# A conditioning vector on its way through DRAM: 1536 single numbers, or 16 rows turned by TensorE

## The chip, the core and the metric

The kernel runs on one core of one Trainium2 chip. The metric is the device time of one execution in microseconds (us); less is better. The engines are TensorE (PE, with its weight loads as PEld), VectorE (DVE), ScalarE (ACT), GpSimd (POOL) and SyncE (SP). SP issues nearly all DMAs here; its entries in a timeline (SPq) are the time that the issue of a DMA took, not the transfer itself.

## The reference, cut to what matters

`x` is 4 batches of 1024 tokens of 512 numbers, `cond` has one row of 128 numbers for each batch.

```python
scale = cond @ norm_w.T + 1.0                       # [4, 512]
ms = jnp.mean(x * x, axis=-1, keepdims=True)
h = x * (scale[:, None, :] * jax.lax.rsqrt(ms + 1e-6))
u = h @ up_w.T                                      # [4, 1024, 4096]
val, gate = jnp.split(u, 2, axis=-1)
h = val * gelu(gate)                                # exact gelu
y = act_quant(h) @ weight_quant(down_w).T           # 8 bits a token; three values
return y + x
```

The change concerns `scale`: how its rows for batches 1 to 3 get from the layout in which they are computed to the layout in which the tokens are multiplied by them.

## The kernel before, in words

Work goes batch by batch, in a schedule written out by hand (`manual_schedule`): each engine carries out its instructions in the order in which the program text issues them, and waits on semaphores where data or a buffer is not ready. The up product is cut into NJ = 16 blocks j of 128 columns of `val` and 128 of `gate`, and into two halves h of 512 tokens.

**The first batch.** `plain_half(j, h)` (line 600) makes one block of one half: 12 matmuls of the gate into a PSUM bank `pg` (line 580), a gelu by ACT (line 604), 12 matmuls of the value into `pv` (line 580), and DVE's product of the two (line 608). `pg` has one bank for h = 0 and two in turn for h = 1; `pv` has two in turn, so a `pv` group waits until DVE's line 608 of two groups before has read the bank. The order of the halves is (1,0), (2,0), (0,1), (1,1), (2,1), and then (3,0), (3,1), (4,0), (4,1) and on to (15,1), by the loop at line 1176, which calls `first_batch(j, sc)` (line 1020).

**Weights on the fly.** Between the halves of block j, the other engines prepare later blocks. `w_range` (line 282) finds a row's power of two on DVE (lines 271, 147, 277, 280); `w_scale` (line 293) scales by it, on ACT from block 3 on (line 298). From block 3 on, `w_rows(n)` (line 317) splits the block into a high and a low f16 part (ACT line 322, DVE line 323) in a slot of the buffer `H`, and SP's transposing DMA of line 324 turns it into the weight tile: one of two tiles in `SXY`, or `S_more`, a part of `R`, for every third block (5, 8, 11, 14). The slot serves again two blocks later: ACT's line 322 of block 7 waits until the transpose of block 5 has been read out. POOL adds the block's quarters for the later batches (`s_sums`, lines 356 to 359), ACT and POOL split the sums (lines 368 and 372), and SP spills them to DRAM (`s_spill`, line 376). In `first_batch(j)` the text order between the halves and after them sets what stands behind what; `w_rows(5)` stands between the halves of j = 3, `w_rows(6)` after its second half, `w_rows(7)` after the second half of j = 4.

**The down weights.** `d_sum` (line 427), `d_mean` (the `pmean` matmul of line 436 at the end of j = 4), `d_round` (DVE, lines 442 and 443) and `d_put` (ACT line 452) quantize `down_w` in the same stretch.

**The conditioning.** `scT` [128, NK, B] holds `scale` with the 512 numbers of a batch as 4 columns (NK = 4) of 128 partitions, for 4 batches (B). Batches 1 to 3 are computed by `cond_scale_rest` (lines 189, 190), `cond_largest` adds 1 (line 194) and finds the largest of each batch, `cond_over` turns these on PE (`pm`, line 203), `cond_range` and `cond_spread` make a power of two of each and spread it over the partitions (`pd`, line 219), and `cond_undo` stores it and its inverse (`dx`, `ux`, lines 223 and 226). This last part, followed by `cond_rows` (line 228), runs in `first_batch(3)`, after its first half and ahead of two `pair_max` on DVE (line 694) and of `w_scale(5)` and `w_rows(5)`. `cond_rows` writes the columns of each batch b to a DRAM tile `rows_dram` [B, 512], one DMA for each batch, 512 runs of 4 bytes in it.

At j = 5, `cond_load_scale(1)` reads the row back, to all 128 partitions (line 236), as tile `sc`; at j = 6 `cond_bring` multiplies it by `ux` (DVE line 240), and the tokens of batch 1 are multiplied by it in the blocks 6 to 13 (`Tokens`: `norm` line 499 and `rsqrt` lines 469 and 470, `scale` lines 507 and 512, `sums` on POOL from line 520, then a split, lines 544 and 548, and a transposing DMA, line 551). The rows of batches 2 and 3 are read the same way at the start of batches 1 and 2, and used on line 240 some blocks later.

**Later batches.** They use 7 products of half the size for 8 (line 565, a Strassen form), with the quantization and the down product of the batch before beside them (line 836).

Of the kernel before, what the change touches and what calls it, by code (L numbers as in the profile page):

```python
# [8 lines left out]
F32 = mybir.dt.float32  # L9
# [9 lines left out]
P = 128  # L19
# [31 lines left out]
def glu_quant_kernel(  # L51
# [10 lines left out]
    PE, ACT, DVE, POOL, SP = nc.tensor, nc.scalar, nc.vector, nc.gpsimd, nc.sync  # L62
    B, S, D = x.shape
# [5 lines left out]
    NK = D // P  # L69
# [6 lines left out]
    sm = ctx.enter_context(tc.tile_pool(name="small", bufs=2))  # L76
# [3 lines left out]
    ident = cpool.tile([P, P], F32, name="ident")  # L80
# [28 lines left out]
    warm = H[:, 9, 0].bitcast(F16)[:, :TOK]  # L109
    DVE.memset(warm, 0.0)  # L110
    am_dram = tc.dram_tile([B, 2 * TOK], F32, name="am_dram")
    rows_dram = tc.dram_tile([B, D], F32, name="rows_dram")

    def t_view(b):
        v = R[:, b % 2].bitcast(F16)[:, : NA * C_ALL * 2 * HALF]
# [33 lines left out]
    def bank(tag, bufs, shape=None, name=None):  # L149
        return psum.tile(shape or [P, TOK], F32, name=name or tag, tag=tag, bufs=bufs)  # L150

    def po_bank(name, shape=None):
        return bank("po", 3, shape, name)


    scT = cpool.tile([P, NK, B], F32, name="scT")
# [70 lines left out]

    def cond_rows():

        for b in range(1, B):  # L230
            SP.dma_start(out=rows_dram[b].rearrange("(k p) -> p k", p=P), in_=scT[:, :, b])

    def cond_load_scale(b):

        sc = wpool.tile([P, D], F32, name=f"sc_{b}", tag="sc", bufs=1)
        SP.dma_start(out=sc, in_=rows_dram[b].partition_broadcast(P))
        return sc

    def cond_bring(b, sc):
# [780 lines left out]
    def first_batch(j, sc):  # L1020
# [19 lines left out]
        if j == 3:  # L1040
            pd = cond_spread(dg, 1, B, "po")
            cond_undo(pd, 1, B)
            cond_rows()
# [132 lines left out]
    for j in range(3, NJ):  # L1176
        if j == 5:
            sc = cond_load_scale(1)
        if j == 6:
            cond_bring(1, sc)  # L1180
        first_batch(j, sc if j >= 5 else None)
# [87 lines left out]
    for b in range(1, B):  # L1269
# [19 lines left out]
        if b + 1 < B:  # L1289
            sc = cond_load_scale(b + 1)  # L1290
            bring = lambda b=b, sc=sc: cond_bring(b + 1, sc)
            steps[1, "z"] = [(bring, (0.4, 0))]
            p0 = b * NJ + 12
            plan = [
                (None, p0, ((6, "z"), (7, "x"), (7, "y"), (9, "y"), (10, "x"), (10, "z"))),
                (p0 + 4, None, ((9, "y"), (10, "x"), (10, "y"), (11, "y"), (12, "x"), (12, "x"))),
                (None, None, ((10, "y"), (11, "x"), (11, "y"), (13, "x"), (13, "y"), (13, "z"))),
                (p0 + 2, p0 + 4, ((9, "z"), (12, "x"), (12, "y"), (14, "x"), (14, "y"), (14, "z"))),
            ]
            for a, (at, nx_at, places) in enumerate(plan):  # L1300
                def make(a=a, at=at, nx_at=nx_at, b=b):
                    toks[a] = Tokens(b + 1, a, at, nx_at)
                    toks[a].load()
                fs = [
                    make,
                    lambda a=a: toks[a].norm(),
                    lambda a=a, sc=sc: toks[a].scale(sc),
                    lambda a=a: toks[a].high(),
                    lambda a=a: toks[a].low(DVE),
                    lambda a=a: toks[a].turn(),  # L1310
                ]
                costs = ((0, 0), (0, 1.6), (0, 1.5), (0, 2.1), (2.6, 0), (0, 0))
                for place, f, c in zip(places, fs, costs):
                    steps.setdefault(place, []).append((f, c))
# [85 lines left out]
    b = B - 1  # L1400
# [159 lines left out]
```

## Time and profile before

| What | us |
|---|---|
| median of 3 runs | 738.65 (738.46 to 740.53) |
| the profiled execution | 738.87 |
| its span, first to last instruction | 737.1 |
| PE busy (matmuls) | 722.0 (98%) |
| DVE, ACT, POOL busy | 596.9, 391.3, 199.0 |
| first batch on PE, `plain_half` and `plain_first` | to 194.25 |
| a group of 12 matmuls of line 580, full clock, start to start | 2.59 |
| rows written, line 231: 3 DMAs of 2 KB, issue to landing | 10.9 |
| `sc` read, line 236: 3 DMAs of 256 KB, issue to landing | 5.4 |

In the chain of work, a view that goes back from the last instruction and notes what released each step, the share of an engine is the time in which it was the one that the end waited for. Where PE is in the chain nearly all the time, another engine's time counts only where PE stands still for it. The table of the page in 40 slices of 18.4 us shows the granted clock of PE (PEclk) in tenths: 9 in 39 slices and 8 in the fifth, 73.7 to 92.1 us. The list of DMA packets gives, for any stretch of time, how many packets started in it and how many of them were small.

### The profile page before, as it was taken

The numbers are of one execution on the slowest core, as the hardware profiler recorded it, in microseconds if no ns is written. First come the engines' busy times: TensorE is split into PE (matmuls) and PEld (weight loads), VectorE is DVE, ScalarE is ACT, GpSimd is POOL, SyncE is SP. The second block draws the span as 40 slices with busy tenths as digits, with TensorE's granted clock in tenths as the row PEclk, the third lists the DMA queues.
The fourth block names the chain that finished last, engine by engine and source line by source line (L and its number), as shares of the span: only waits on it lengthen the run. The fifth ranks groups of instructions, "written<-read, shape, count | busy, mean of one in ns | idle before, by whom it ended". The sixth has DMA issues, their size and how long they took to land.

```text
span 737.1 us, 10140 instructions
## 1 busy us (share of the span) xinstructions
PE 722.0 (98%) x3660; PEld 359.2 (49%) x3660; DVE 596.9 (81%) x827; ACT 391.3 (53%) x629; POOL 199.0 (27%) x207
## 2 busy tenths in 40 slices
PE   7998799999999999999999999999999999999998
PEld 3544344444444445665444445666444444445844
DVE  6978889876979889797689897787678888764897
ACT  6868476665235676534334666453433666332274
POOL 1379757896110030460010030452020000000100
PEclk9999899999999999999999999999999999999999
DMA  6659999998434646866944556766934565453263
GB/s 239 242 181 206 277 243 235 260 262 221 150 87 106 134 106 155 196 150 180 223 105 101 99 131 171 157 152 162 225 101 103 103 106 107 102 104 97 86 187 114
DMA packets 204382, 117.30 MB, mean 159 GB/s; under 512 B 166950, under 2 KB 174503, under 8 KB 204332
## 3 DMA queue, kind: packets, MB, share of 16 engines
q1 hardware_dynamic: 204042, 116.33, 64.9%
q8 instruction: 28, 0.46, 0.3%
q10 hardware_dynamic: 290, 0.33, 0.1%
q14 instruction: 22, 0.18, 0.1%
HBM read 54.22 MB, written 23.09 MB: 105 GB/s over the span
## 4 chain that ended last, share of the span: by engine, by line
PE 90%; DMA 3%; DVE 2%; POOL 2%; ACT 1%; issue 1%; SPq 0%; DVEq 0%; POOLq 0%; ACTq 0%
PE A L565 34%; PE E L565 17%; PE B L565 8%; PE po L836 8%; PE pg L580 8%; PE pv L580 7%; PE po_end L785 4%; DMA R<-H 2%; PE po L785 1%; DMA H<-in_x_dram 1%; DMA SXY<-H 1%; POOL R L372 1%; PE po_B L836 0%; PE ptx L926 0%; PE pv L623 0%
## 5 line engine op out<-in xcount | busy, mean ns | idle before, releaser
L565 PEld LDWEIGHTS <-SXY 128*128 128x128 f16 x2016 | 197.3, 98 | 232.3 <-issue 0.6
L565 PE MATMUL A<-R,SXY 128*128 128x512 f16 x1152 | 266.2, 379 | 0.0
L565 PE MATMUL E<-R,SXY 128*128 128x512 f16 x576 | 140.0, 379 | 0.1
L663 DVE SCALAR_TENSOR_TENSOR H<-A,sg,t 128x512 f32<-128x512 f32 x48 | 36.0, 750 | 72.9 <-PE A L565 72.7
L715 POOL PARTITION_ALL_REDUCE am<-R x8 | 14.4, 1795 | 232.2 <-DVE R L701 232.2
L757 DVE TENSOR_TENSOR H<-H,am 128x1024 f32<-128x1024 f32 x64 | 76.2, 1217 | 0.0
L580 PEld LDWEIGHTS <-SXY 128*128 128x128 f16 x486 | 47.3, 98 | 58.1 <-DMA SXY<-H 0.8
L676 ACT ACTIVATE t<-t,sg 128x512 f32<-128x512 f32 x48 | 34.6, 721 | 70.7 <-DVE t L673 70.6
L565 PE MATMUL B<-R,SXY 128*128 128x512 f16 x288 | 70.0, 379 | 0.0
L699 DVE TENSOR_REDUCE gm<-H 128x512 f32<-128x1024 f32 x56 | 69.0, 1232 | 1.0
L580 PE MATMUL pg<-R,SXY 128*128 128x512 f16 x252 | 57.8, 379 | 0.3 <-DMA SXY<-H 0.3
L836 PE MATMUL po<-wd,R 128*128 128x256 fp8e4 (+1 forms) x448 | 56.8, 275 | 0.0
L580 PE MATMUL pv<-R,SXY 128*128 128x512 f16 x234 | 54.4, 379 | 0.4 <-DVE H L608 0.4
L836 PEld LDWEIGHTS <-R 128*128 128x128 bf16 (+1 forms) x480 | 46.9, 98 | 12.8
L660 ACT ACTIVATE t<-B,sg 128x512 f32<-128x512 f32 x48 | 33.0, 688 | 35.8 <-PE B L565 35.8
L469 POOL TENSOR_SCALAR ssq<-ssq 128x2 f32<-128x2 f32 x12 | 3.6, 299 | 176.7 <-ACT xt L499 124.0
L643 ACT COPY t<-A 128x512 f32<-128x512 f32 x48 | 28.0, 583 | 39.8 <-PE A L565 39.5
L651 ACT COPY B<-A 128x512 f32<-128x512 f32 x48 | 27.4, 572 | 39.0 <-PE A L565 38.5
L765 ACT ACTIVATE H<-H 128x1024 f32<-128x1024 f32 x38 | 39.9, 1050 | 14.2 <-DVE H L757 14.1
L655 ACT COPY v<-E 128x512 f32<-128x512 f32 x48 | 28.1, 586 | 31.6 <-PE E L565 27.8
L580 PEld LDWEIGHTS <-R 128*128 128x128 f16 x258 | 25.6, 100 | 37.2 <-DMA R<-H 6.0
L701 DVE TENSOR_TENSOR R<-R,gm 128x512 f32<-128x512 f32 x56 | 42.6, 762 | 1.3
(203 smaller groups left out, 999.1 us busy)
## 6 DMA issues: line engine op xcount, KB each, us to landing
SXY<-s_dram SPq DMA_DIRECT2D x57, 256.0 KB, 3.2
s_dram<-SXY SPq DMA_DIRECT2D x18, 384.0 KB, 3.2
H<-in_L_cond_up_w_dram SPq DMA_DIRECT2D x13, 512.0 KB, 5.1
SXY<-s_dram SPq DMA_DIRECT2D x39, 128.0 KB, 3.3
xr<-in_x_dram SPq DMA_DIRECT2D x19, 256.0 KB, 3.6
out_dram<-xr SPq DMA_DIRECT2D x19, 256.0 KB, 2.5
H<-in_x_dram SPq DMA_DIRECT2D x8, 512.0 KB, 6.7
R<-in_L_cond_down_w_dram SPq DMA_DIRECT2D x8, 512.0 KB, 7.3
```

The lines of the kernel that those rows point to most:

```text
L565: PE.matmul(o, s[:, w, k, :], tv[:, :, c, l, k, :], start=start and n == 0, stop=stop and n == len(TERMS) - 1, skip_group_check=True,)
L580: PE.matmul(ps, a[k // 2][:, w, k % 2, :], XP[:, l, k, h * TOK : (h + 1) * TOK], start=n == 0, stop=n == len(terms) - 1,)
L655: ACT.copy(cur["v"], cur["E"])
L660: ACT.activation(cur["t1"], pb, AF.Gelu, scale=gain(g, 1))
L663: DVE.scalar_tensor_tensor(h_half(g - 1, 0), prev["A"], gain(g - 1, 0), prev["t1"], ALU.mult, ALU.mult)
L676: ACT.activation(prev["t2"], prev["t2"], AF.Gelu, scale=gain(g - 1, 1))
L699: DVE.tensor_reduce(gm[0], v, AX.X, ALU.max, apply_absolute_value=True)
L701: return [largest, lambda: DVE.tensor_tensor(m, m, gm[0], ALU.max)]
L757: DVE.tensor_tensor(v, v, r.to_broadcast([P, 2, TOK]), ALU.mult)
L765: ACT.activation(v, v, AF.Copy, bias=MAGIC)
L785: PE.matmul(po.rearrange("p (y c o) -> p y c o", c=2, o=P), q[:, a, h, j], wd8[:, :, j // n, j % n, :, y0:y1].rearrange("p c o y -> p y c o"),
L836: PE.matmul(po, w[:, j], m, start=start and j == 0, stop=stop and j == n - 1, skip_group_check=True,)
```

## The change

`cond_rows` no longer writes columns. PE turns `scT`, seen as [128, 16] (column k * B + b), into [16, 128] in a PSUM bank of the kind `po` (three in turn); DVE copies it to SBUF; SP writes it with one DMA, 16 rows of 512 bytes. `rows_dram` has the shape [16, 128] for it, and the load of a batch takes its four rows of 128 numbers to each partition, 4 runs of 512 bytes where one of 2048 was. The place in the program, the numbers and everything after the load are as before; the column of batch 0 goes along and is not read.

```diff
-    rows_dram = tc.dram_tile([B, D], F32, name="rows_dram")
+    rows_dram = tc.dram_tile([NK * B, P], F32, name="rows_dram")
...
     def cond_rows():
 
-        for b in range(1, B):
-            SP.dma_start(out=rows_dram[b].rearrange("(k p) -> p k", p=P), in_=scT[:, :, b])
+        pr = po_bank("pr", [NK * B, P])
+        PE.transpose(pr, scT.rearrange("p k b -> p (k b)"), ident)
+        rows = sm.tile([NK * B, P], F32, name="rows", bufs=1)
+        DVE.tensor_copy(rows, pr)
+        SP.dma_start(out=rows_dram, in_=rows)
 
     def cond_load_scale(b):
 
         sc = wpool.tile([P, D], F32, name=f"sc_{b}", tag="sc", bufs=1)
-        SP.dma_start(out=sc, in_=rows_dram[b].partition_broadcast(P))
+        SP.dma_start(
+            out=sc.rearrange("p (k q) -> p k q", k=NK),
+            in_=rows_dram.rearrange("(k b) q -> b k q", b=B)[b].partition_broadcast(P),
+        )
         return sc
```

## The prediction

> **What bounds the kernel now.** I read the page's chain of work first, then the waits, the timeline of the stretch they point to, then the DMA packets in it. The chain's share by engine:
>
> ```profile
> PE 90%; DMA 3%; DVE 2%; POOL 2%; ACT 1%; issue 1%; SPq 0%; DVEq 0%; POOLq 0%; ACTq 0%
> ```
>
> TensorE (PE) sets the end, so only time in which it stands or runs slowly can be won. The list of PE's waits names one of size:
>
> ```profile
> PE pg L580 <- DMA R<-H: 5.9, 1, 5.9
> PE pv L580 <- DVE H L608: 0.4, 1, 0.4
> ```
>
> The chain in order of time (start, us, what) shows that wait. The DMA is the transposing one of line 324, which `w_rows(5)` issues; before and after, PE's groups of 12 matmuls take 2.59:
>
> ```profile
> 63.88 0.95 PE pv L580 x5
> 64.84 12.82 DMA R<-H
> 77.66 0.04 issue
> 77.70 4.63 PE pg L580 x12
> 82.33 2.59 PE pv L580 x12
> ...
> 103.09 0.70 ACT g L604
> 103.79 0.01 issue
> 103.80 1.23 DVE xn L512
> ```
>
> PE had finished everything older at 71.77 (the `pmean` matmuls, 71.49 + 0.28) and stood 5.93 until 77.70. The windows by time give a granted clock of 0.50 from 75 to 81, back at 1.00 from 82: the first group after the wait took 4.63, 2.04 more than its neighbours. The episode costs PE 5.93 + 2.04 = 7.97 us. Another transpose on this line, from 45.93, lies 4.37 long in the chain; why did this one take 12.82? SP's queue shows what went just ahead, and what SP then did:
>
> ```profile
> 63.03 1.69 SPq L231 DMA_DIRECT2D rows_dram<-scT  x3
> 64.84 2.98 SPq L324 DMA_TRANSPOSE R<-H  x1
> 67.92 1.00 SPq L376 DMA_DIRECT2D s_dram<-SXY  x2
> 69.01 0.41 SPq L376 DMA_DIRECT2D s_dram<-R  x1
> 69.53 10.48 SPq L324 DMA_TRANSPOSE SXY<-H  x1
> ```
>
> The three writes of the rows are the change's subject. The DMA packets of three single microseconds, 58 to 59 (an undisturbed transpose), 66 to 67 and 69 to 70:
>
> ```profile
> DMA packets 1001, 0.26 MB, mean 256 GB/s; under 512 B 1001, under 2 KB 1001, under 8 KB 1001
> ...
> DMA packets 1924, 0.13 MB, mean 125 GB/s; under 512 B 1911, under 2 KB 1911, under 8 KB 1924
> ...
> DMA packets 31, 0.01 MB, mean 8 GB/s; under 512 B 31, under 2 KB 31, under 8 KB 31
> ```
>
> The small packets pass in the microsecond from 66; afterwards the transpose, which had run at 1001 packets per us, crawls at 31 to 163 from 68 to 74 and recovers at 74 to 75 (675). The row of the writes says 10.9 us from issue to landing: 64.22, the last one's issue, + 10.9 = 75.1, where the crawl ends. So I hold the 1536 four-byte writes to DRAM for its cause. Against "any small packets do this": reading `am_dram` back as single numbers puts 790 small packets into 242 to 243, and those reads land in 3.1 us.
>
> **The change, part by part.** Blocks are written (j, half).
>
> Removed: three writes, 1.69 us of SP, 1536 packets. Added on PE: one f32 transpose behind the `pd` matmuls at 55.63. The row of `pm` on line 203, of the same kind, has 0.27 and 0.42; I take 0.3. It waits for nothing (`scT` is final at 39.04). Added on DVE: one copy of 16x128 out of PSUM behind `dx` (61.22). Rows around it: a COPY of 128x3 at 0.13, a 3x128 reduction out of PSUM at 0.27, a TENSOR_SCALAR of 128x12 at 0.34; no row is of its kind, so 0.13 to 0.34, and I take 0.27. Its wait on PE is over by 56.4, five us before DVE comes there; behind it stand the two L694 and L323 of w_rows(5), and with L323 the transpose at 64.84, which DVE released (L323 ended at 64.77; SP was free at 64.73). So transpose (5) goes out at 65.1, not earlier, although SP has 1.2 us less to issue. DVE then idled 1.25 before 66.69, so the copy's cost ends there. The write's wait on the copy (done near 61.7) is over before SP is through with line 263 at 62.99.
>
> The write of 16 rows has no row: from below 2.0 us to landing (128 KB of results), from above 10.9. Its only reader is the load at 91.25, over 20 us later: nothing, either way. The three loads of `sc` fall from 128 packets of 2048 bytes to 512 of 512. Between the rate of 256-byte packets (256 GB/s, 58 to 59) and of 2048-byte ones (395, 84 to 85) 256 KB take 1.02 or 0.66 us: 0 to 0.4 more on the first load (nearer 0.2); the others are issued far ahead of their use (the last at 363.7, line 240 at 382.8).
>
> Here the skill speaks against the change. "DMA: Bandwidth & Descriptors", section "Why small descriptors are slow (HBM only)", charges a packet some 3 extra cycles and 32 bytes of metadata; by that alone 1536 packets over 16 engines are gone in well under a microsecond, and removing them would save about that. The packets did pass in about one microsecond here, but the rows show eight more during which others stood. "Specifications" of the same page puts full rate at 512 bytes and up; by it the loads lose nothing.
>
> Now the saving. Transpose (5) issued at 65.1 + 4.4 (median landing of line 324) = 69.5, before PE's 72.1 (71.77 + 0.3). PE's wait and the slow clock go: 7.97 - 0.3 = 7.7 at most. **What is late next** decides how much stays. I replay the engines' orders with their own row durations.
>
> ACT's L322 of w_rows(7) waited for the same landing (77.73 after 4.73 idle): it now starts at 73.05, ends 74.1. DVE's L323 (7), at 78.81 after 1.68 idle, starts when L438 ends at 77.14, ends 78.4; what follows on DVE moves 1.7. POOL's sums (L356 to L359, ending 76.79) did not depend on PE, so ACT's L368 (6) goes to 75.7, POOL's L372 from 79.59 to 76.8. ACT's two L452 wait for the rounding on DVE (L443), the second until 83.8; then come g (5,1) at 84.9 (87.55 before), L368, L298, and L322 (8) ending 88.95 (91.57). DVE's L323 (8) follows and ends at 90.7, not 93.3. Before, DVE then stood 2.92 for `sc`, until 96.23. On SP, transpose (6) no longer blocks 10.48 (others 1.9 to 4.9), SP is free by 73 to 75, and transpose (7) goes out behind L323 (7), at 78.45 and not 83.61. With the same issue times behind it, the load of `sc` moves from 91.25 to 86.1 and lands (4.98, plus up to 0.4) at 91.1 to 91.5; with a shorter issue of (7), earlier. So `cond_bring` on line 240 starts between 90.7 and 91.5: 5.5 to 4.7 earlier, 5.3 taken. From there DVE is busy to L512 (103.80), POOL takes it up at 105.10 after 8.35 idle, and the chain runs POOL, ACT, DVE to L608 (9,0) and PE's 134.53: all of it 5.3 earlier. PE comes out of its lead: it now waits about 1.7 at pv (6,0) for L608 (5,0) (85.6 + 0.74), and again near 112 and 129; there it stands where the chain lets it, 5.3 earlier than before. After 134.53 PE waits 0.6 in all in the old trace, so the shift reaches the end. The other loss of the old wait, 2.4 us, is given back to that chain.
>
> Sum: the profiled execution took 738.87 (span 737.1 and 1.77 around it); 738.87 - 5.3 = 733.6. It lies 0.22 above the median of the runs (738.65), so 733.4.
>
> **Rivals.** (a) The chain behind it is looser than my replay (POOL's and DVE's durations vary between 0.72 and 1.2 for one form): then PE's own rate binds, 738.65 - 7.7 = 731.0. For it: PE waited 0.39 for others in the whole stretch; against it: the chain of 103 to 134. (b) The chain is tighter: only ACT's 2.65 at g (5,1) survives, because `sc` lands late or the DMA queue, busy to the full around 85 to 105, moves its work less: 738.65 - 2.65 = 736.0. (c) The change doesn't do what it says: the crawl has another cause (two transposes and three spills in flight), or 16 rows hold up the queue as well. Then the wait stays and 0.3 on the transpose's issue is added: 739. Against it: none of this line's 12 other transposes shows more than about 1 us of such a crawl in its packets, and it ends where the writes land. (d) Slower: PE's new waits between 84 and 130 each drop the clock as the old one did. The episode at 0.50 lasted some 6.8 us (0.3 of the microsecond from 74 by its 0.84, six full ones, 0.5 of the one from 81 by its 0.74), worth 3.4 at most; it must first use up the 2.4 of slack and the 5.3, so it decides from three episodes on (10.2), and four give 738.65 - 7.7 + 13.6 = 744.6. Against it: the wait of 1.6 ahead of the `ptx` matmuls at 10.6 left the clock at 1.00, and none of the new ones in the replay is longer than 1.7.
>
> **How the numbers follow.** Forecast, 732.5 to 734.8: 0.55. (a), 730.9 to 732.5: 0.14. (b), 734.8 to 736.8: 0.22. (c): 0.06. (d): 0.03. A difference of 0.3%, 2.2 us, is about what a measurement of this kernel can tell from none, so faster means under 736.4: 0.55 + 0.14 + 0.20 = 0.89; same 0.08 ((c) and the end of (b)); slower 0.03. The range takes (a) and (b) up to their own prices: 731.0 to 736.2.
>
> **What would show it.** Right: no PE wait on `R<-H`, the clock at 1.00 from 74 to 82, transpose (5) landing in 4 to 6, no one-microsecond window under 200 packets between 67 and 72 while a transpose is out, transpose (6) issued in under 5; line 240's start near 91; PE waits on L608 of 1 to 2 near 85 and a smaller one near 129. Wrong: a wait on `R<-H` that stays (c); PE unbroken from 72 to 195 (a); line 240 at 93 or later (b); clock below 1 after 84 (d).

## The result, and the profile after

| | before | after |
|---|---|---|
| median (lowest to highest) of 11 runs each | 738.61 (737.21 to 740.85) | 736.39 (735.1 to 737.82) |
| ratio | | 0.9967, interval 0.9953 to 0.9982 |
| the profiled execution, its span | 738.87, 737.1 | 735.1, 733.3 |

The change makes the kernel 2.2 us faster. The forecast was 733.4, and 736.39 lies 0.2 above the range's upper end. The profiled execution of after is the fastest of its eleven; profile against profile the gain is 3.8. So there are two things to explain: why 3.8 and not 5.3, and why 2.2 in the medians.

Lines of the changed kernel are 6 higher from line 237 on (L324 is now L330, L240 is L246, L608 is L614, L512 is L518); `rows` is copied on L233, written on L234 and read back on L239. The chain of work by engine, and the granted clock, on the page of after:

```profile
PEclk9999999999999999999999999999999999999999
...
PE 84%; DVE 9%; ACT 2%; issue 2%; POOL 1%; DMA 1%; SPq 0%; DVEq 0%; ACTq 0%
```

The fifth slice is at 9 now, so the slow clock after the wait is gone. PE's share of the chain fell from 90 to 84 and DVE's rose from 2 to 9: in a stretch DVE has become the engine that the end waits for. PE's waits (in total, times, longest) say where:

```profile
PE pv L586 <- DVE H L614: 2.9, 3, 1.8
...
PE pmean L442 <- DVE wpart L437: 0.8, 1, 0.8
```

No wait on `R<-H` is left. Three new ones on DVE's line 614 stand in its place (0.74 ahead of 86.74, 1.78 ahead of 114.64, 0.38 ahead of 130.72). SP's timeline shows that the transposes are free:

```profile
63.25 0.44 SPq L234 DMA_DIRECT2D rows_dram<-rows  x1
66.42 1.89 SPq L330 DMA_TRANSPOSE R<-H  x1
...
70.63 3.46 SPq L330 DMA_TRANSPOSE SXY<-H  x1
```

Transpose (6) blocks SP for 3.46 instead of 10.48. The packets of two microseconds, 68 to 69 and 69 to 70, belong to transpose (5); there is no crawl (before: 51 and 31):

```profile
DMA packets 833, 0.21 MB, mean 213 GB/s; under 512 B 833, under 2 KB 833, under 8 KB 833
...
DMA packets 832, 0.21 MB, mean 212 GB/s; under 512 B 832, under 2 KB 832, under 8 KB 832
```

Where did the rest of the gain stay? Two timelines of after side by side, first DVE (start, us), then POOL in the same stretch:

```profile
87.38 2.02 DVE L449 TENSOR_SCALAR R<-R 128x1024 f32<-128x1024 f32 x1
89.32 0.74 DVE L614 SCALAR_TENSOR_TENSOR H<-pv,sg,g 128x512 f32<-128x512 f32 x1
89.98 1.71 DVE L329 TENSOR_TENSOR H<-H 128x1024 f16<-128x1024 f32 x1
91.62 0.95 DVE L246 TENSOR_SCALAR sc<-sc,ux 128x512 f32<-128x512 f32 x1
```

```profile
86.64 2.22 POOL L378 TENSOR_TENSOR SXY<-H,SXY 128x768 f16<-128x768 f32 x1 [1.88 <-ACT SXY L374]
...
90.58 1.71 POOL L363 TENSOR_TENSOR H<-H 128x256 f32<-128x256 f32 x1
```

And the same two DVE lines before:

```profile
88.72 0.69 DVE L443 TENSOR_SCALAR R<-R 128x1024 f32<-128x1024 f32 x1
...
96.23 0.49 DVE L240 TENSOR_SCALAR sc<-sc,ux 128x512 f32<-128x512 f32 x1 [2.92 <-DMA sc<-rows_dram]
```

The rounding took 0.69 when it began ahead of POOL (whose L372 started at 89.03), and takes 2.02 behind POOL's 2.22, which began at 86.64. The multiplication of `sc` took 0.49 and takes 0.95 behind POOL's 1.71. It no longer waits for `sc`: it follows L329 without a pause, so DVE's own work is what sets it.

### The profile page after: what moved, and what is told of

Read it like the earlier page. It is cut to its first block, busy times and chain, and to the rows that moved or that the text cites. A ratio compares the mean times of both kernels' runs of the same rounds, so it can differ in the third digit from the quotient of the medians.

```text
span 733.3 us, 10144 instructions
## 1 busy us (share of the span) xinstructions
PE 721.2 (98%) x3661; PEld 358.5 (49%) x3661; DVE 600.6 (82%) x828; ACT 390.9 (53%) x629; POOL 200.1 (27%) x207
## 4 chain that ended last, share of the span: by engine, by line
PE 84%; DVE 9%; ACT 2%; issue 2%; POOL 1%; DMA 1%; SPq 0%; DVEq 0%; ACTq 0%
PE A L571 34%; PE E L571 17%; PE B L571 8%; PE po L842 8%; PE pv L586 5%; PE pg L586 5%; PE po_end L791 4%; DVE H L614 1%; DVE H L329 1%; DVE wam L277 1%; PE po L791 1%; DVE R L448 1%; DMA H<-in_x_dram 1%; DVE gm L705 1%; DVE nx L554 1%
## 5 line engine op out<-in xcount | busy, mean ns | idle before, releaser
L688 DVE SCALAR_TENSOR_TENSOR H<-v,sg,t 128x512 f32<-128x512 f32 x48 | 36.6, 762 | 7.4 <-ACT t L682 7.4
```

The costliest lines, as they stand in the source:

```text
L688: DVE.scalar_tensor_tensor(h_half(g - 1, 1), prev["v"], gain(g - 1, 0), prev["t2"], ALU.mult, ALU.mult)
```

## The experiments

Executions start differently: the first loads land earlier or later, and PE's wait ahead of the `ptx` matmuls (1.4 in the profile of after, up to 3.4 in others) carries that on. To compare one profile with another I use the time from the start of PE's group (3,0), which lies ahead of what nearly all variants change, to the end of DVE's last instruction, with which the chain ends. It is 683.95 before and 680.02 after.

**1. Before again, unchanged.**

> The kernel before, unchanged, to see its own executions one by one: span and granted clock of each. Theory A (the missing part of the gain is the new copy on DVE): executions near 738.6, all with a clock near 0.995, as the profiled one, and a wait on R<-H of 5 to 6 in the profile. Rival B (the profiled execution of before was a dear one: how long the clock stays low differs from execution to execution): times spread over 737.2 to 740.9 with the clock, from 0.998 down to 0.991, and the cheapest executions are those with the shortest low clock. Rival C (the changed kernel's new waits lower its clock): says nothing on this run.

Measured: 739.02 (12 runs), ratio 0.9993 (0.9981 to 1.0005). Its profile starts 1.16 later, at (3,0) in 51.51 and not 50.35, and still has the span 737.0:

```profile
PE pg L580 <- DMA R<-H: 4.6, 1, 4.6
PE ptx L926 <- DVE wam L147: 2.6, 1, 2.6
```

PE leaves the wait at 77.50, against 77.70 in the first profile. The transpose, from 66.09 to 77.46, was 11.37 long here and 12.82 there. From (3,0) to the end it is 682.68, 1.27 less. The shorter crawl is 0.61 of that: DVE's line 512 (`xn`), through which the chain runs, starts 52.84 after (3,0) here and 53.45 there. The other 0.66 is a wait of PE near 330, of 0.6 on line 836, which the first profile has and this one lacks. Behind `xn`, fourteen of the seventeen profiles take 630.46 to 630.63 to the end, and the three without that wait (this one and those of runs 8 and 14) 629.70 to 629.85. Two differences between executions are mixed here, then, and `xn` shows the crawl alone.

The equal span in spite of the late start doesn't show that the old wait swallows one. The transpose went out 14.58 after (3,0) here and 14.49 there, so its issue moved with the start, and what made up for it is the shorter crawl and the missing wait. Run 7, which has the crawl too, starts 1.95 later than the first profile and has a span 1.9 longer.

**2. No turn and no copy.** The write takes 16 rows of the identity, so the scales of batches 1 to 3 are left out.

```diff
-        pr = po_bank("pr", [NK * B, P])
-        PE.transpose(pr, scT.rearrange("p k b -> p (k b)"), ident)
-        rows = sm.tile([NK * B, P], F32, name="rows", bufs=1)
-        DVE.tensor_copy(rows, pr)
-        SP.dma_start(out=rows_dram, in_=rows)
+        SP.dma_start(out=rows_dram, in_=ident[: NK * B])
```

> The change without its turn: the one write of 16 rows of 512 bytes takes the identity's first 16 rows, PE's transpose and DVE's copy are left out, so batches 1 to 3 get wrong scales; everything else as in the changed kernel. Theory A (the copy on DVE and what it shifts cost about 0.9): cond_bring on DVE starts near 90.7 instead of 91.6, the transpose of block 5 goes out near 65.0 instead of 66.4, median about 0.9 below the changed kernel, 735.5. Rival C (clock lowered by PE's new waits): same time as the changed kernel, 736.4, within 0.4, and the clock below 1 in about two executions of three.

Measured: 735.36 (8 runs), ratio 0.9943 (0.9923 to 0.9963); 679.68 from (3,0). The turn and the copy together cost 0.34 by that measure, and 0.34 at `xn` too (49.20 after (3,0) and not 49.54; the profiles of the change and of runs 5, 8 and 12 to 15 lie between 49.54 and 49.62). The median is 1.0 lower, as far as the expectation had it, but it says more of the starts: 2 of these 8 executions have a mean clock of 0.998 or less, and 5 of the change's 11.

**3. The copy on ACT.**

```diff
-        DVE.tensor_copy(rows, pr)
+        ACT.copy(rows, pr)
```

> The changed kernel with the copy of the 16 rows out of PSUM on ACT instead of DVE. Theory A: ACT has room there (it idles before w_rows(7) and later), so it runs like the kernel without the turn: 735.5 to 735.9, transpose of block 5 out near 65.2. Rival C: 736.4, as the changed kernel.

Measured: 736.87 (9 runs), ratio 0.995 (0.9932 to 0.9968); 679.74 from (3,0), 0.28 less than the change. The median doesn't show it: this profile had a start gap of 2.68 and a clock of 0.5 for 3.41 from 12.87 on.

**4. The turn, the copy and the write early:** the call leaves `first_batch(3)` and stands ahead of the loop, behind the `pm` matmul at about 39.

```diff
-            cond_rows()
...
+    cond_rows()
```

> The changed kernel with the turn, the copy and the write of the rows moved up to just behind the pm transpose (they need scT alone, which is ready at 39), where DVE idles 2.2 and 2.6 before 49. Theory A: the copy costs nothing there; transpose of block 5 out near 65.0, cond_bring near 90.7, median 735.5. Rival C: 736.4, as the changed kernel.

Measured: 736.69 (8 runs), ratio 0.9954 (0.9936 to 0.9971); 679.65 from (3,0), and the same kind of start (gap 2.26, clock 0.5 for 6.83 from 12.47 on). Runs 2 to 4 agree: taking the copy off DVE's way gives about 0.3, so it is not where 1.4 to 2.6 us of the forecast went.

**5 and 6. Twice the idle matmuls at the start,** in the changed kernel and in the one before.

```diff
-    keep_warm(7)
+    keep_warm(14)
```

> The changed kernel with 14 instead of 7 idle matmuls on PE behind the pd matmul of the start, in PE's gap from 9.3 to 10.7 (up to 11.8 in executions whose first loads land late). Theory D (executions of both kernels sometimes drop the clock near 12.5, behind that gap, which costs 1.3 to 2.5; without such a drop the change gains 3.5): clock 1.0 in nearly all executions, median 735.4. Rival E (what hurts is the late landing of the first loads, which the old wait on the transpose swallowed and the changed kernel pays): the median stays near 736.4, with a clock of 1.0 all the same.

Measured: 735.98 (735.28 to 736.35, 5 runs), ratio 0.9956 (0.994 to 0.9971), every run with a mean clock of 1.0; 680.05 from (3,0).

> The kernel before with the same 14 idle matmuls. Theory D: clock 0.995 (the drop behind the wait on the transpose stays) in nearly all executions, none at 0.993 or lower, median 738.6 to 738.9, 3.3 above the changed kernel with them. Rival E: 738.9 as well, but then 2.4 above the changed kernel with them.

Measured: 738.96 (11 runs), ratio 0.9995 (0.9983 to 1.0007); 682.79 from (3,0), PE's wait on `R<-H` 4.20. With 14 idle matmuls in both, 3.0 separate the medians of the two. The changed kernel's median goes from 736.39 to 735.98. The old one's stays (738.70 beside it with 7), although none of its 11 executions has a mean clock below 0.995; why it gains nothing is open.

**7. The change, with three writes of single numbers put back,** to a DRAM tile that nobody reads.

```diff
+        for b in range(1, 4):
+            SP.dma_start(out=junk_dram[b].rearrange("(k p) -> p k", p=P), in_=scT[:, :, b])
```

> The changed kernel, and behind its one write of the rows the three old writes of columns, 1536 numbers of 4 bytes, to a DRAM tile that nobody reads. Theory A (these writes alone hold up the transposing DMA): the transpose of block 5 lands 11 to 13 after its issue, PE waits 4 to 7 on R<-H, the clock falls, 738.5 to 739.5. Rival F (the crawl came of the turn of other DMAs in flight): no wait on R<-H, the time of the changed kernel.

Measured: 740.81 in one run. PE's wait, and SP's queue:

```profile
PE pg L589 <- DMA R<-H: 5.4, 1, 5.4
```

```profile
65.55 1.53 SPq L237 DMA_DIRECT2D junk_dram<-scT  x3
67.19 1.92 SPq L333 DMA_TRANSPOSE R<-H  x1
...
71.39 10.20 SPq L333 DMA_TRANSPOSE SXY<-H  x1
```

The packets from 70 to 71:

```profile
DMA packets 39, 0.01 MB, mean 10 GB/s; under 512 B 39, under 2 KB 39, under 8 KB 39
```

The wait, the crawl and the clock of 0.5 for 6.83 are back as they were, and from (3,0) it took 684.00, like the kernel before. The rest of the 740.81 is a late start (ahead of `ptx` a wait of 2.52, then a clock of 0.5 for 3.41). So it was these writes.

**8. The same 1536 packets of 4 bytes to SBUF instead.**

```diff
+        for b in range(1, B):
+            SP.dma_start(out=junk_sb[:, b, :, 0], in_=scT[:, :, b])
```

> The changed kernel, and behind its one write of the rows three DMAs with the same source columns, 1536 packets of 4 bytes again, but to a strided tile in SBUF. Theory A1 (it is single numbers written to DRAM that back up): the packets pass in a microsecond or so, the transpose of block 5 lands 4 to 6 after its issue, no wait on R<-H, 735 to 736.5. Rival A2 (so many packets of 4 bytes hold up the queue wherever they go): a wait on R<-H of 4 to 7, 738.5 to 739.5.

Measured: 734.44 in one run, no wait on `R<-H`. The packets from 66 to 67 and from 68 to 69:

```profile
DMA packets 1647, 0.09 MB, mean 86 GB/s; under 512 B 1596, under 2 KB 1612, under 8 KB 1647
...
DMA packets 830, 0.21 MB, mean 212 GB/s; under 512 B 830, under 2 KB 830, under 8 KB 830
```

As many small packets, and the transpose behind them at its full rate. The number of packets is not the cause. In SBUF the numbers lie 8 bytes apart, four to a partition, so this run alone doesn't tell DRAM from lying side by side; runs 11 to 15 go on from there.

**9. DVE relieved: the change with 14 idle matmuls, the copy and the `sc` multiplication of batch 1 on ACT.**

```diff
-        DVE.tensor_copy(rows, pr)
+        ACT.copy(rows, pr)
...
-        DVE.tensor_scalar(sc, sc, ux[:, b : b + 1], None, ALU.mult)
+        if b == 1:
+            ACT.activation(sc, sc, AF.Copy, scale=ux[:, b : b + 1])
+        else:
+            DVE.tensor_scalar(sc, sc, ux[:, b : b + 1], None, ALU.mult)
```

The call of `cond_bring(1, sc)` moved behind the first tokens' `norm` and `d_put` of j = 6, and `keep_warm(14)` as in run 5.

> The changed kernel with the copy of the rows on ACT, the multiplication of sc for batch 1 (line 246) on ACT behind the first tokens' norm and d_put of j = 6, and 14 idle matmuls at the start. Theory (DVE is the engine that gave part of the gain back: its rows between L329(7) and xn L518 grew by 1.2 to 1.9 us where they now run beside POOL): with 0.95 of L246 and 0.27 of the copy taken from DVE, xn comes 0.5 to 1.2 earlier, end less start of group (3,0) 679.0 to 679.6 (after_warm 680.05), 734.7 to 735.5, no slow clock at the start. Rival (sc's landing and the chain over POOL and ACT set xn, DVE has room there): within 0.2 of after_warm, end less (3,0) 679.9 to 680.2, 735.8 to 736.2.

Measured: 734.65 (734.47 to 735.36, 5 runs), ratio 0.994 (0.9925 to 0.9954); 679.33 from (3,0), 0.72 less than run 5. The DVE timeline where L246 had stood:

```profile
90.14 1.72 DVE L332 TENSOR_TENSOR H<-H 128x1024 f16<-128x1024 f32 x1
91.78 1.21 DVE L280 TENSOR_REDUCE wam<-H 128x2 f32<-128x1024 f32 x1
```

The reduction follows at once, without L246's 0.95 between, and `xn` starts 48.86 after (3,0) (99.52 - 50.66) instead of 49.55 in run 5 (101.24 - 51.69). So DVE's work sets `xn`, and half of what the replay missed comes back when some of it is taken away. Line 332 still takes 1.72 beside POOL. This version is 4.4 us under the 739.03 of before beside it. Its median lies 1.3 under that of run 5, measured on another chip; the intervals of the two ratios overlap.

**10. The old writes kept, only later:** the kernel before, with the call moved from between the halves of j = 3 to after the second half of j = 4, ahead of `w_scale(7)`, where transposes (5) and (6) are already out.

```diff
-            cond_rows()
...
+        if j == 4:
+            cond_rows()
```

> The old 1536 four-byte writes, only moved: issued after the second half of j = 4, ahead of w_scale(7) and w_rows(7), some 10 us later, behind transposes (5) and (6). Theory (the four-byte writes hold up whatever is behind them on the queue for some 9 to 10 us, and the cost depends only on what is due then): no wait of PE on R<-H at (4,1), transpose (5) lands in 4 to 6; the crawl moves to some 10 us from about 75 to 78, transpose (7) lands late (over 8 us), its weights are due only at group (7,1) near 110, so PE doesn't wait for it; the load of sc goes out behind it and lands 0 to 3 later than in the changed kernel: 735.4 to 737.0, end less (3,0) 679.9 to 681.5. Rival (the loss is of the writes themselves, wherever they are, or transposes are always tight): a wait of PE of 3 or more somewhere between 75 and 115 on H or SXY, 738 to 740.

Measured: 738.79 (12 runs), ratio 1.0002 (0.9987 to 1.0016). My theory gave 735.4 to 737.0, and failed in one step. The wait on `R<-H` is gone, as it said, and the crawl moved:

```profile
77.12 2.29 SPq L231 DMA_DIRECT2D rows_dram<-scT  x3
79.86 9.49 SPq L324 DMA_TRANSPOSE SXY<-H  x1
...
92.17 0.51 SPq L236 DMA_DIRECT2D sc<-rows_dram  x1
```

But SP stands 9.49 on transpose (7), and the load of `sc`, behind it on the queue, goes out at 92.17, and not at 86.09 as in the changed kernel. DVE pays for it:

```profile
97.68 0.49 DVE L240 TENSOR_SCALAR sc<-sc,ux 128x512 f32<-128x512 f32 x1 [5.93 <-DMA sc<-rows_dram]
```

PE then waits 8.7 in six pieces for DVE's line 608 (3.42 the longest). Removing PE's wait alone was worth nothing; the load of `sc` sets the end through DVE, as the prediction's chain had it.

**11 to 15. What sets the length of the crawl?** Each is the change with one added write to an unread DRAM tile where the old writes stood; only the number of the numbers and their distance differ. Run 11 writes the 512 numbers of batch 1 as the old kernel did, run 12 only its first 128:

```diff
+            SP.dma_start(out=junk_dram[b].rearrange("(k p) -> p k", p=P), in_=scT[:, :, b])
...
+        SP.dma_start(out=junk_dram[1].rearrange("(k p) -> p k", p=P)[:, 0:1], in_=scT[:, 0:1, 1])
```

Runs 13 and 14 write the 512 numbers into the first column of a tile of 512 rows, with 16 numbers to a row (13) or 128 (14); run 15 writes all of `scT` in runs of 4 numbers:

```diff
+        SP.dma_start(out=junk_dram.rearrange("(k p) q -> p k q", p=P)[:, :, 0], in_=scT[:, :, 1])
...
+        SP.dma_start(out=junk_dram.rearrange("k p b -> p k b"), in_=scT)
```

> The changed kernel with one added column write of 512 four-byte numbers to a DRAM tile that nobody reads, where the old ones were. Theory (crawl in proportion to the number of four-byte packets to DRAM): a crawl of about 3 us in place of 9 to 10, transpose (5) lands some 7 to 8 after its issue near 65.5, that is at 72.5 to 74, PE waits 0.5 to 2 on R<-H, span 733.5 to 736. Rivals: all or none: a crawl of 8 to 10 as with three writes, PE waits 4 to 6, span 737 to 739; or a threshold below which nothing happens: landing in 4 to 5, no wait, span 733 to 734.8.

> The changed kernel with one added write of only 128 four-byte numbers (512 contiguous bytes) to a DRAM tile that nobody reads. One write of 512 numbers gave a PE wait of 4.5 us, three of them 5.4: not in proportion. Theory S (a fixed hold-up once single numbers are written to DRAM): crawl of 5 to 8 us, PE waits 3.5 to 5 on R<-H, span 735 to 737. Theory L (numbers of one stretch of DRAM go one after another, the rows of three batches side by side, so the length goes with the numbers of one row, 8.6 us / 512 = some 16 ns each): 128 numbers hold up about 2 us, transpose (5) lands at 70 to 72, no wait of PE or below 0.5, span 732.5 to 734.5.

> The changed kernel with one added write of 512 four-byte numbers, 64 bytes apart in DRAM instead of next to each other (an unread tile of 32 KB). Theory L (numbers that share a small stretch of DRAM wait for each other): no crawl or one below 2 us, no PE wait on R<-H, span 732.5 to 734.5. Theory N (each four-byte write to DRAM costs the same wherever it goes): as with 512 numbers side by side, PE waits 3.5 to 5.5 on R<-H, span 735 to 737.

> As spread64, 512 bytes apart (an unread tile of 256 KB). Theory L with a stretch of up to 512 bytes: here no crawl and no wait, span 732.5 to 734.5, also if 64 bytes apart still showed one. Theory N: PE waits 3.5 to 5.5 on R<-H, span 735 to 737.

> The changed kernel with one added write of all of scT as 512 runs of 16 bytes, lying next to each other, to an unread DRAM tile of 8 KB. If the size of the single write is what matters below 64 bytes (whatever its neighbours do): 512 packets as with one column write, PE waits 3.5 to 5.5 on R<-H, span 735 to 737. If L holds and what counts is how many writes fall into one 64-byte stretch (4 here, 16 before): a crawl of about a quarter, 1.5 to 3 us, PE wait 0 to 1, span 732.5 to 735.

| Run | written to DRAM | wait on `R<-H` | issue of transpose (5) to PE's start | time, one run |
|---|---|---|---|---|
| 7 | 3 x 512 numbers, side by side | 5.4 | 67.19 to 79.27: 12.1 | 740.81 |
| 11 | 512 numbers, side by side | 4.5 | 65.24 to 76.66: 11.4 | 737.77 |
| 12 | 128 numbers, side by side | 1.2 | 66.66 to 74.47: 7.8 | 735.38 |
| 13 | 512 numbers, 64 bytes apart | none | none to wait for | 735.55 |
| 14 | 512 numbers, 512 bytes apart | none | none to wait for | 735.06 |
| 15 | 512 runs of 16 bytes, side by side | none | none to wait for | 738.4 |

The packets of one microsecond in which a transpose is out, for run 11 (70 to 71), 13 (69 to 70) and 15 (72 to 73):

```profile
DMA packets 43, 0.01 MB, mean 11 GB/s; under 512 B 43, under 2 KB 43, under 8 KB 43
```

```profile
DMA packets 852, 0.22 MB, mean 218 GB/s; under 512 B 852, under 2 KB 852, under 8 KB 852
```

```profile
DMA packets 824, 0.21 MB, mean 211 GB/s; under 512 B 824, under 2 KB 824, under 8 KB 824
```

Run 15's time is not due to its write: PE's wait ahead of `ptx` was 3.4 there, with a clock of 0.5 for 3.41 behind it, and from (3,0) it took 680.05, like the change itself. So in these runs the crawl needs single numbers that lie next to each other in DRAM. It grows with the numbers of one row (128 to 512) and little with the number of rows (one to three), which I had not expected before run 11: there I had put a third of three. Why neighbours hold each other up, these runs don't say. That the writes to one small stretch go one after another fits runs 11 to 14 and is an inference; by it run 15, with four writes to 64 bytes, should have shown about a quarter of the crawl, and shows none: transpose (6) issues in 3.47 there, 3.46 in the changed kernel.

## Why the prediction missed, step by step

**What held.** The cause: the 1536 four-byte writes to DRAM make the transposes behind them crawl (runs 7, 8, 11 to 14). The wait on `R<-H` and the clock at 0.50 are gone. The copy lasts 0.27, as taken. The load of `sc` goes out at 86.09, forecast 86.1, and that is luck: transpose (7) ahead of it went out 1.3 late (79.76, forecast 78.45) and issued 1.4 faster than before (3.51 and 4.92). Transpose (6) issues in 3.46, forecast under 5. PE does wait for L614 near 85, 112 and 129. The clock stays at 1.00 through these waits of up to 1.78, so rival (d) is out; (c) is out by run 7; (a) is out because PE is not unbroken. Line 246 comes at 91.62, before rival (b)'s mark of 93, while the median lies inside (b)'s prices: the size came out there, by another mechanism than the late `sc` that (b) named.

**The step that failed: "I replay the engines' orders with their own row durations."** Rows of DVE keep their durations only beside the same neighbours and in the same order. In the old trace DVE stood 1.68 ahead of L323 (7) and 0.79, 0.65 and 2.92 between it and L240; once these waits are filled, the same instructions run at other moments against POOL. The 28 instructions from the L323 of w_rows(7) up to `xn` kept DVE busy 12.86 + 7.37 before (the split is at line 240) and 13.45 + 8.03 after: 1.3 us more for the same work. Not every row grew: one rounding went from 0.69 to 2.02, L323 (7) from 1.23 to 1.74, line 240 from 0.49 to 0.95, and the first L442 fell from 2.13 to 1.15. Counted from (3,0), line 240's move is 45.88 to 41.16, 4.7 (forecast 5.3, and 4.7 was its late end), and that of `xn` 53.45 to 49.54, 3.9. The 3.9 reach the end unchanged (683.95 to 680.02). On PE's side the 7.97 were won as forecast, and its four new waits give back 3.68 (0.78, 0.74, 1.78, 0.38) where the sum had 2.4. Run 9 takes the copy and the `sc` multiplication off DVE and gets 0.72 back.

The step before it failed in the same way: transpose (5) was to go out at 65.1 and went out at 66.42, since L329 took 2.51 instead of 1.21. POOL ran beside it in both traces, first before, then after:

```profile
63.54 2.75 POOL L372 TENSOR_TENSOR SXY<-H,SXY 128x768 f16<-128x768 f32 x1 [1.07 <-ACT SXY L368]
63.56 1.21 DVE L323 TENSOR_TENSOR H<-H 128x1024 f16<-128x1024 f32 x1
...
63.62 1.64 POOL L378 TENSOR_TENSOR SXY<-H,SXY 128x768 f16<-128x768 f32 x1 [1.09 <-ACT SXY L374]
63.83 2.51 DVE L329 TENSOR_TENSOR H<-H 128x1024 f16<-128x1024 f32 x1
```

Before, the two began within 0.02 of each other and POOL's was the long one; behind the copy DVE came 0.21 later, and its own was. PE paid 0.78 for it ahead of `pmean`, since DVE's `wpart` came later, and had it back at its next wait, 0.74 here against 1.78 in run 2.

Here a rule of the Trainium skill explains the rows. "SBUF — State Buffer", section "Who interferes with whom", says that DVE and GpSimd share a pair of ports that one of them holds for a whole instruction while the other blocks. It names a copy or scalar operation of DVE in a two-port mode, and one with two inputs in SBUF, but not a reduction. This trace agrees. In the profile of after, a TENSOR_SCALAR of 128x1024 numbers takes 0.69 to 0.75 where POOL stands still (8 rows) and 0.74 to 2.02 where a POOL instruction had begun ahead of it (7 rows); the TENSOR_TENSOR above took 1.21 and 2.51; the 15 TENSOR_REDUCE of line 277 take 1.20 to 1.21 beside POOL and without. The replay would have had to count POOL as a neighbour of such rows. That POOL lengthens them is read from the rows; no run takes POOL's work away.

**"The copy's cost ends there"** (in the idle 1.25 before 66.69): run 2 gives 0.34 for turn and copy that do reach the end. Small.

**The base of the sum: 738.87 - 5.3 from one execution.** That execution's crawl was long: `xn` starts 53.45 after (3,0), against 52.84 and 52.29 in the profiles of runs 1 and 6. It also started earlier than run 1, at 50.35 against 51.51, and its total lay near the median all the same. That was luck, and the forecast took it for a usual execution. Against the other two the change, with its 49.54, gains 3.3 and 2.7, close to the 3.0 of runs 5 and 6.

The rest, down to 2.2 in the medians, lies at the start. In the change's eleven runs, those at 735.1 to 735.62 have a mean clock of 1.0 and those at 736.11 to 737.82, the median among them, have 0.997 to 0.999; the profiles of runs 3, 4 and 15 show such a loss as 3.41 or 6.83 us at 0.5 from about 12.5 on. The six of the eleven at 0.999 or more average 735.7. The old kernel pays for such a start as well: of 68 executions of it (run 1 and those timed beside runs 1 to 10), the 20 with a mean clock below 0.995 average 740.6 and the other 48 738.8. Of 36 of the changed kernel and of runs 2 to 4, the 17 at 0.998 or less average 737.3 and the other 19 735.3. A slow start costs both about the same, 1.8 and 2.0, so the old wait had not been covering it. Executions without one differ by about 3.1 (738.8 and 735.7).

**What stays open.** Such slow stretches at the start came somewhat more often in the changed kernels, though the change's first instruction comes some 40 us later: by these counts in 17 of 36 and in 20 of 68 (the old wait alone leaves 0.995). Why, and whether the two shares really differ, no run tells apart. With 14 idle matmuls none was seen in 5 and 5 runs of the changed forms.

## What to carry to other kernels

Ahead of time-critical transfers, don't write single numbers side by side to DRAM: turn them on the chip, or write runs of 16 bytes or more (one run here had them, without a hold-up). When a long wait goes, replay what comes next with the durations that its rows have beside their new neighbours (here DVE behind POOL: up to three times as long), and read the price from more than one execution. Before calling two executions alike, compare them piece by piece: equal totals hid a shorter crawl, a missing wait and a later start. Once the wait is gone, the next term of the chain (here DVE) is where to go on.

## What the runs showed of the hardware

- 512 four-byte numbers written side by side to DRAM pass the queue within a microsecond, and the queue behind them then passes 26 to 113 packets in each microsecond from 69 to 73 (run 11), where transposes pass 824 to 852 undisturbed (runs 8, 13 and 15). The same numbers 64 bytes apart (run 13), 1536 such packets to SBUF, 8 bytes apart (run 8), or runs of 16 bytes (run 15) brought no wait. "DMA: Bandwidth & Descriptors" of the Trainium skill, section "Why small descriptors are slow (HBM only)", prices small packets by their number; runs 11 and 13 have the same 512 and differ by a wait of 4.5 us.
- PE's clock dropped to 0.5 for 3.41 or 6.83 after waits of 2.26, 2.52, 2.68 and 3.36 near the start (runs 4, 7, 3 and 15), and for 3.41 in run 12 after two waits of 0.81 and 1.2 with 0.4 of work between. It did not drop after 2.08 and 2.14 in runs 13 and 14, after 2.62 in run 1, nor after 3.42 at 100.73 in run 10. So the length of a wait alone doesn't decide it here. "TensorE: Matmul & The Clock Gate", section "What's actually happening", has a free-running window of 3.413 us, which the lengths agree with (one and two of it). The limit of about 3.4 us for a harmless gap, in its section "HAM oscillation — how this bites in real kernels", is too wide for this kernel.
